# A selective scan's operands: the state as the inner partition index, and dt stored beside dt times x

## The chip, the cores and the metric

The kernel runs on one core of one Trainium2 chip. The metric is device time in microseconds (us) from one launch to its end; the median of the runs is given. Engine names are those of the profile: PE is the matrix engine (PEld its weight loads), DVE the vector engine, ACT the scalar engine, POOL the general-purpose engine, SP the engine whose queue issues nearly all DMAs here.

## The reference, cut to what matters

Two layers work on x of 4 batches by 48 x 48 tokens by 128 channels, all in float32. The first is a two-dimensional selective scan. After a group norm, an input projection to 256 channels, a 3 x 3 depthwise convolution and a SiLU, the tokens are scanned in K = 4 directions (rows, columns, and both backwards), with N = 16 states for each channel:

```python
x_dbl = jnp.einsum('bkdl,kcd->bkcl', xs, x_proj_w)
dts_r, Bs, Cs = (x_dbl[:, :, :R], x_dbl[:, :, R:R + N], x_dbl[:, :, R + N:])
dts = jnp.einsum('bkrl,kdr->bkdl', dts_r, dt_proj_w)
dt = jax.nn.softplus(dts + dt_proj_b[None, :, :, None])
A = -jnp.exp(A_logs).reshape(K, d, N)
...
def step(h, inp):
    dt_l, u_l, B_l, C_l = inp
    dA = jnp.exp(dt_l[..., None] * A)
    h = h * dA + (dt_l * u_l)[..., None] * B_l[:, :, None, :]
    y = jnp.einsum('bkdn,bkn->bkd', h, C_l)
    return (h, y)
```

The four directions' y are added, normed, gated and projected back to 128 channels. The second layer is an attention of the 2304 tokens with themselves, and then a mixture of four spectral convolutions over time (16 filters, the "STU").

## The kernel before, in words

**Tiling of the scan.** One batch is 4 directions x 6 chunks of CS = 384 tokens, 24 chunks (`Chunk`, L327). In a chunk, 256 channels x 16 states = 4096 scans are to be made. They are cut into 8 units (`Unit`, L437): h in 0..1 is the half of the channels, q in 0..3 a group of four states. A unit is a tile s of 128 partitions x 4 groups g x 384 tokens. Its 128 partitions are C4 = 4 states (c) times DL = 32 channels (j), and g runs over four sets of 32 channels. In the kernel before, partition p is c * 32 + j: the state is the outer index.

**Operands of a unit.** A channel's dt and dt * x are needed on four partitions, one for each state c; a state's B and C are needed on 32 partitions, one for each channel j. They are spread so:

- `prep` (L348) projects x to xd (dt's low-rank part, B, C), computes dt by a matmul and a softplus into re[:, h, 0] (L389, L397), multiplies by x into re[:, h, 1] (L414), and writes re out to a DRAM tile dtdud: `store(h)` (L401) issues four DMAs, one for each g, each of 32 partitions. dtdud is laid out as half, channel j, dt or dt * x, group g, token.
- `load(h)` (L405) reads dtdud back into the tile rep, with four DMAs, one for each state c, each writing 32 neighbouring partitions with all that a channel j has: 2 x 4 x 384 values, 12 KB in one run.
- `fetch` (L429) reads one row of xd, which was written to DRAM (xdd, L392), into 32 neighbouring partitions of a tile bc, four DMAs for a tile. C is always spread this way, and B for the units that POOL enters.
- For the other units PE spreads B: `spread` (L445) multiplies xd by a matrix of ones and zeros, made once at L119 to L125.

**A unit's work.** `enter` (L451) makes s = rep[:, 1] * B, on DVE for five of the eight units and on POOL for three. `scan` (L459) does, for each g, dA = exp(A * dt) on ACT (L464) and the scan on DVE (L467). `times_c` (L470) multiplies by C on POOL. `sum_c` (L478) sums the four states of each channel by a matmul with csum, a 128 x 32 matrix made at L128.

**What sets the order.** The kernel is issued in an order written out by hand. `scans` (L518) goes over the 192 units of a batch; unit by unit it enters the next units, gives 15 steps of `prep` for chunks up to three ahead, and lets other work run in between in proportion to its columns of matmul: for batch 0 the mixing of the filters' weights (`mixture`, L813), and for batches 1 to 3 the STU of the batch before (`stu`, L908). That work reads large tiles tt of filter values (L954) and G of weights (L965). Between two scan stages come the scan's epilogue, the attention, and the next batch's projection and convolution. After batch 3 its STU runs alone. `begin_scans` (L502) prepares a batch's first chunk ahead of its stage. Nearly all DMAs are issued by SP, in the order of the program. They use eight completion semaphores in turn, and a DMA waits until the earlier user of its semaphore has landed, so that at most eight are under way. The tile rep has three buffers, each bc tile one, tt four.

Of the kernel before, what the change touches and what calls it, by code (L numbers as in the profile page):

```python
# [8 lines left out]
F32 = mybir.dt.float32  # L9
AF = mybir.ActivationFunctionType  # L10
ALU = mybir.AluOpType
AX = mybir.AxisListType
# [3 lines left out]
P = 128  # L16
# [3 lines left out]
D, NS, R, K = 256, 16, 8, 4  # L20
NH = D // P
CS = 384
SUB = 384
NT = L // P
G4, DL, C4, Q4 = 4, 32, 4, 4
# [29 lines left out]
def hybrid_kernel(ctx: ExitStack, tc: tile.TileContext, a: dict, out: bass.AP):  # L55
# [3 lines left out]
    nc = tc.nc  # L59
    ctx.enter_context(tc.manual_schedule())  # L60
    wp = ctx.enter_context(tc.tile_pool(name="w", bufs=1, side="left"))
    keep = ctx.enter_context(tc.tile_pool(name="keep", bufs=1, side="left"))
    res = ctx.enter_context(tc.tile_pool(name="res", bufs=1, space=DRAM))
    dram = ctx.enter_context(tc.tile_pool(name="dram", bufs=3, space=DRAM))
    bank = {}

    ident = wp.tile([P, P], F32, name="ident")
# [48 lines left out]
    onerow = wp.tile([P, 1], F32, name="onerow")  # L116
    nc.vector.memset(onerow, 0.0)

    spread = wp.tile([P, 2, Q4, C4, DL], F32, name="spread")  # L119
    nc.vector.memset(spread, 0.0)  # L120
    for v in range(2):
        nc.gpsimd.affine_select(onerow, onerow, pattern=[[0, 1]], compare_op=ALU.not_equal, fill=1.0,
                                base=-R - 64 * v, channel_multiplier=1)
        nc.gpsimd.affine_select(spread[:, v], spread[:, v], pattern=[[-C4, Q4], [-1, C4], [0, DL]],
                                compare_op=ALU.not_equal, fill=1.0, base=-32 - 64 * v, channel_multiplier=1)  # L125

    csum = wp.tile([P, DL], F32, name="csum")
    nc.vector.tensor_reduce(csum, ident.rearrange("p (c j) -> p j c", j=DL), AX.X, ALU.add)  # L128
    shift = wp.tile([P, 1], F32, name="shift")
    nc.vector.memset(shift, -SHIFT)  # L130
    carry = wp.tile([P, NH, Q4, G4], F32, name="carry")
# [36 lines left out]
    def prologue(b, pool, mm_tile):  # L168
# [116 lines left out]
        for i in range(n):  # L285
            enter(i)
# [30 lines left out]
    def in_order(t, k, lo, n):  # L317

        if k % 2 == 0:
            return t[:, lo // W:(lo + n) // W, :]  # L320
        return t.rearrange("p h w -> p w h")[:, lo // H:(lo + n) // H, :]

    def mm_tile(name):
        pool, tag = bank["mm"]
        return pool.tile([P, 512], F32, tag=tag, name=name)

    class Chunk:  # L327
# [20 lines left out]
        def prep(self, pool):  # L348

            k, name, xc = self.k, self.name, xcs[self.b]
            xdd_ = xdd[k % 2][self.lo // CS]

            def rest(n=1):

                yield
                yield 0  # L360
                yield
                for i in range(3 * n - 3):
                    yield 0 if i % 3 == 1 else None

            if k >= 2:
                xd = self.xd = pool.xd.tile([P, CS], F32, tag="xd", name=f"xd{name}")
                nc.sync.dma_start(xd, xdd_)
            yield from rest(2)
            yield
            if k < 2:  # L370
                xd = self.xd = pool.xd.tile([P, CS], F32, tag="xd", name=f"xd{name}")
                ps = mm_tile(f"xp{name}")
                for h in range(NH):
                    nc.tensor.matmul(ps[:, :CS], xw[:, h, k, :], in_order(xc[h], k, self.lo, CS),
                                     start=(h == 0), stop=(h == NH - 1))
            yield 2 * CS if k < 2 else 0
            yield
            if k < 2:
                nc.scalar.activation(xd, ps[:, :CS], AF.Identity, bias=onerow)
            yield from rest()  # L380

            re = pool.one.tile([P, NH, 2, CS], F32, tag="re", name=f"re{name}")
            for h in range(NH):
                yield
                ps = mm_tile(f"dt{name}_{h}")
                nc.tensor.matmul(ps[:, :CS], dtw[:, k, h * P:(h + 1) * P], xd, start=True, stop=True)
                yield CS
                yield
                nc.scalar.copy(re[:, h, 0], ps[:, :CS])  # L389
                if h == 0:  # L390
                    if k < 2:
                        nc.sync.dma_start(xdd_, xd)  # L392
                    yield from rest()
            yield from rest()
            yield

            nc.scalar.activation(re[:, :, 0], re[:, :, 0], AF.Softplus)  # L397
            yield 0
            d = dram.tile([NH, DL, 2, G4, CS], F32, tag="dtdu", name=f"dtdud{name}")

            def store(h):  # L401
                for g in range(G4):
                    nc.sync.dma_start(d[h, :, :, g], re[g * DL:(g + 1) * DL, h])

            def load(h):  # L405
                rep = pool.rep.tile([P, 2, G4, CS], F32, tag="rep", name=f"rep{name}_{h}")
                for c in range(C4):
                    nc.sync.dma_start(rep[c * DL:(c + 1) * DL], d[h])
                self.rep.append(rep)

            for h in range(NH):
                x = in_order(xc[h], k, self.lo, CS)
                dt, dx = [re[:, h, i].rearrange("p (r w) -> p r w", w=x.shape[2]) for i in range(2)]
                nc.vector.tensor_tensor(dx, dt, x, ALU.mult)  # L414
            yield
            yield
            store(0)
            yield 0
            store(1)
            yield  # L420
            yield from rest(2)
            load(0)
            yield from rest(2)
            yield
            yield 0
            load(1)
            yield

        def fetch(self, i, pool):  # L429

            t = self.bc[i] = pool.one.tile([P, CS], F32, tag=f"bc{i}", name=f"bc{self.name}_{i}")
            src = xdd[self.k % 2][self.lo // CS]
            for c in range(C4):
                row = 64 * (self.k // 2) + 32 + 4 * i + c
                nc.sync.dma_start(t[c * DL:(c + 1) * DL], src[row].partition_broadcast(DL))

    class Unit:  # L437

# [6 lines left out]
        def spread(self, ps):  # L445

            self.bt = ps.tile([P, 512], F32, tag="B", name=f"B{self.name}")
            nc.tensor.matmul(self.bt[:, :CS], spread[:, self.ch.k // 2, self.q].rearrange("p c j -> p (c j)"),  # L448
                             self.ch.xd, start=True, stop=True)

        def enter(self, pool):  # L451

            full = self.full = pool.tile([P, G4, CS + 1], F32, tag="s", name=f"s{self.name}")
            s = self.s = full[:, :, self.ch.at]
            bt = self.ch.bc[self.q] if self.pool else self.bt[:, :CS]
            eng = nc.gpsimd if self.pool else nc.vector
            eng.tensor_tensor(s, self.ch.rep[self.h][:, 1], bt.unsqueeze(1).to_broadcast([P, G4, CS]), ALU.mult)  # L457

        def scan(self, g, dAs):  # L459
            ch = self.ch  # L460
            if g == 0:
                nc.scalar.copy(self.full[:, :, ch.slot], none if ch.first else carry[:, self.h, self.q])
            dA = dAs[g % 2]
            nc.scalar.activation(dA[:, 1:CS + 1], ch.rep[self.h][:, 0, g], AF.Exp,  # L464
                                 scale=A[:, ch.k, self.h * G4 + g, self.q:self.q + 1])
            s = self.full.rearrange("p g t -> p (g t)")[:, ch.scanned(g)]
            nc.vector.tensor_tensor_scan(s, dA[:, CS + 1:0:-1] if ch.rev else dA[:, :CS + 1], s, 0.0,  # L467
                                         ALU.mult, ALU.add)
# [49 lines left out]
    def scans(b, chunks, preps, front, sp, back, work, work_cols):  # L518
# [41 lines left out]
        for t in dAs:  # L560
            nc.vector.memset(t[:, 0:CS + 2:CS + 1], 0.0)
        spread(0)
        enter(-2)
        enter(-1)
        spread(1)
        for s in range(len(units) + 2):
            real = s < len(units)
# [340 lines left out]
    def stu(b, pool, ps):  # L908
# [162 lines left out]
        def ended(n, p, lo, hi):  # L1071
            t = now.pop(("T", n - KF + 1))[:hi - lo]
            nc.vector.tensor_tensor(t, t, p[:hi - lo], ALU.add)
            nc.sync.dma_start(out[b, 4 * lo:4 * hi].rearrange("(p j) c -> p j c", j=4), t)

        fetch(0, convs)
        for n, (_, k) in enumerate(items):
            if k == 0:
                begin(n)
            for i, (c, g) in enumerate(convs):  # L1080
                yield from conv(n, c, g)
                fetch(n, convs[i:])
                if i == 0:
                    fetch_G(n)
                elif i == 2 and n > 0:
                    yield from project(n - 1)
                elif i == 5 and k == 0:
                    if n > 0:
                        yield from end(n - 1)
                    yield from ar(n)  # L1090
# [157 lines left out]
```

## Time and profile before

| What | us |
|---|---|
| median of 3 runs | 6303.13 (6301.25 to 6308.65) |
| the profiled execution | 6311.58 |
| its span, first to last instruction | 6309.8 |
| PE busy | 5345.6 (85%) |
| DVE busy | 4482.0 (71%) |
| POOL busy | 3639.1 (58%) |
| ACT busy | 3039.2 (48%) |
| first scan stage, with the mixing of weights | about 140 to 1165 |
| scan stages mixed with the STU | about 1440 to 2540, 2840 to 3960, 4260 to 5370 |
| closing stage, STU alone | about 5660 to 6309 |

A busy time is the sum of an engine's instructions; it doesn't say which engine a stage waits for. The stages have different limits, so they are read one by one. In the whole program the DMA queue that SP feeds moved 1020.80 MB in 652032 packets, and the packets' time is 62.6% of 16 DMA engines over the span. In a line of waits, "A <- B: 30.4, 12, 5.2" says that A's engine sat idle until B for 30.4 us in all, 12 times, at the longest 5.2 us. The chain that ended last is followed back from the last instruction, each step to what released it.

### The profile page before, as it was taken

The numbers are of one execution on the slowest core, as the hardware profiler recorded it, in microseconds if no ns is written. First come the engines' busy times: TensorE is split into PE (matmuls) and PEld (weight loads), VectorE is DVE, ScalarE is ACT, GpSimd is POOL, SyncE is SP. The second block draws the span as 40 slices with busy tenths as digits, with TensorE's granted clock in tenths as the row PEclk, the third lists the DMA queues.
The fourth block names the chain that finished last, engine by engine and source line by source line (L and its number), as shares of the span: only waits on it lengthen the run. The fifth ranks groups of instructions, "written<-read, shape, count | busy, mean of one in ns | idle before, by whom it ended". The sixth has DMA issues, their size and how long they took to land.

```text
span 6309.8 us, 75729 instructions
## 1 busy us (share of the span) xinstructions
PE 5345.6 (85%) x24776; PEld 3339.5 (53%) x24776; DVE 4482.0 (71%) x5563; ACT 3039.2 (48%) x6429; POOL 3639.1 (58%) x1825
## 2 busy tenths in 40 slices
PE   3666666797999998888999998888999998889999
PEld 1222222444556666545555666545555666558889
DVE  6898989558889997458898997458889997311000
ACT  2665666245656654245555654245556654232111
POOL 1888888306788886206787886206788887200000
PEclk6877777799999999899999999899999999899999
DMA  4556555127888888128888888128888888026546
GB/s 100 133 142 148 143 141 143 41 57 179 204 208 222 222 223 236 48 64 192 196 216 209 222 225 230 45 64 194 194 216 214 221 227 236 30 65 159 159 140 215
DMA packets 658249, 1028.95 MB, mean 163 GB/s; under 512 B 93856, under 2 KB 515872, under 8 KB 633248
## 3 DMA queue, kind: packets, MB, share of 16 engines
q1 hardware_dynamic: 652032, 1020.80, 62.6%
q10 hardware_dynamic: 5824, 3.30, 0.2%
q8 instruction: 198, 3.24, 0.2%
q14 instruction: 195, 1.60, 0.1%
HBM read 905.79 MB, written 117.98 MB: 162 GB/s over the span
## 4 chain that ended last, share of the span: by engine, by line
PE 46%; DVE 20%; DMA 18%; ACT 5%; issue 4%; SPq 3%; POOL 3%; DVEq 0%; ACTq 0%; POOLq 0%
PE cv L984 21%; DVE s L467 8%; DMA tt<-fd 7%; PE pr L1050 5%; DVE s L457 4%; PE y L484 4%; PE s L726 3%; DMA rep<-dtdud 3%; DMA G<-gd 3%; PE o L719 3%; DMA bc<-xdd 3%; PE op L662 2%; PE B L448 2%; POOL s L476 2%; DVE xc L266 2%
## 5 line engine op out<-in xcount | busy, mean ns | idle before, releaser
L467 DVE TENSOR_TENSOR_SCAN s<-dA,s 128x385 f32<-128x385 f32 x3072 | 2761.5, 944 | 335.9 <-ACT dA L464 334.5
L476 POOL TENSOR_TENSOR s<-s,bc 128x1536 f32<-128x1536 f32 x768 | 2440.1, 3179 | 194.5 <-DVE s L467 107.6
L464 ACT ACTIVATE dA<-rep,A 128x384 f32<-128x384 f32 x3072 | 1780.1, 585 | 1289.3 <-DVE s L467 1256.2
L984 PE MATMUL cv<-tt,u 128*128 128x256 f32 (+3 forms) x7680 | 1656.8, 355 | 160.3 <-DMA tt<-fd 90.5
L984 PEld LDWEIGHTS cv<-tt,u 128*128 128x128 f32 x7680 | 1271.9, 193 | 662.1 <-issue 292.1
L457 POOL TENSOR_TENSOR s<-rep,bc 128x1536 f32<-128x1536 f32 x288 | 994.1, 3452 | 95.7 <-DMA bc<-xdd 95.7
L457 DVE TENSOR_TENSOR s<-rep,B 128x1536 f32<-128x1536 f32 x480 | 833.9, 1737 | 107.5 <-PE B L448 72.4
L984 PE MATMUL cv<-tt,us 128*128 128x256 f32 (+3 forms) x3840 | 862.5, 353 | 21.6 <-DMA tt<-fd 20.6
L484 PE MATMUL y<-s,csum 128*32 128x384 f32 x6144 | 722.0, 545 | 108.5 <-DVE ya L490 73.4
L984 PEld LDWEIGHTS cv<-tt,us 128*128 128x128 f32 x3840 | 646.9, 193 | 221.7 <-issue 82.9
L1013 DVE TENSOR_TENSOR U<-cv,Q 128x256 f32<-128x256 f32 (+1 forms) x640 | 245.5, 384 | 688.1 <-PE cv L984 678.5
L1050 PE MATMUL pr<-U,G 128*128 128x288 f32 (+7 forms) x2048 | 596.1, 422 | 11.0 <-DMA G<-gd 9.3
L448 PE MATMUL B<-xd,spread 128*128 128x384 f32 x960 | 443.7, 547 | 182.6 <-DVE s L457 170.6
L1010 ACT COPY U<-cv 128x256 f32<-128x256 f32 (+1 forms) x640 | 223.3, 349 | 643.6 <-PE cv L984 642.9
L475 POOL COPY carry<-s 128x4 f32<-128x4 f32 x640 | 121.4, 190 | 680.5 <-DVE s L467 652.2
L1050 PEld LDWEIGHTS pr<-U,G 128*128 128x128 f32 x2048 | 339.9, 192 | 158.6 <-issue 81.5
L998 ACT COPY Q<-cv 128x256 f32<-128x256 f32 (+3 forms) x640 | 223.4, 349 | 387.2 <-PE cv L984 384.8
L726 PE MATMUL s<-xnT 128*128 128x512 f32 (+1 forms) x720 | 357.8, 582 | 42.7 <-ACT xnT L688 23.4
L728 ACT ACTIVATE e<-s,shift 128x512 f32<-128x512 f32 (+1 forms) x360 | 231.2, 644 | 314.2 <-PE s L726 313.7
L160 POOL TENSOR_TENSOR ln_vu<-ln_vu,mhalf 128x4 f32<-128x4 f32 (+1 forms) x20 | 26.8, 1341 | 602.0 <-DVE ln_vu L159 602.0
L484 PEld LDWEIGHTS y<-s,csum 128*32 128x32 f32 x6144 | 127.3, 112 | 461.5 <-issue 333.4
L719 PE MATMUL o<-e,xn 128*128 128x512 f32 (+1 forms) x720 | 343.6, 560 | 4.5 <-ACT e L728 4.5
(161 smaller groups left out, 3722.7 us busy)
## 6 DMA issues: line engine op xcount, KB each, us to landing
rep<-dtdud SPq DMA_DIRECT2D x768, 384.0 KB, 7.6
tt<-fd SPq DMA_DIRECT2D x192, 577.0 KB, 5.2
bc<-xdd SPq DMA_DIRECT2D x2304, 48.0 KB, 3.4
tt<-fd SPq DMA_DIRECT2D x192, 513.0 KB, 4.8
tt<-fd SPq DMA_DIRECT2D x192, 385.0 KB, 4.5
dtdud<-re SPq DMA_DIRECT2D x768, 96.0 KB, 2.2
G<-gd SPq DMA_DIRECT2D x192, 256.0 KB, 5.6
tt<-fd SPq DMA_DIRECT2D x64, 514.0 KB, 5.9
```

Of the source, the lines that this page charges most:

```text
L448: nc.tensor.matmul(self.bt[:, :CS], spread[:, self.ch.k // 2, self.q].rearrange("p c j -> p (c j)"), self.ch.xd, start=True, stop=True)
L457: eng.tensor_tensor(s, self.ch.rep[self.h][:, 1], bt.unsqueeze(1).to_broadcast([P, G4, CS]), ALU.mult)
L464: nc.scalar.activation(dA[:, 1:CS + 1], ch.rep[self.h][:, 0, g], AF.Exp, scale=A[:, ch.k, self.h * G4 + g, self.q:self.q + 1])
L467: nc.vector.tensor_tensor_scan(s, dA[:, CS + 1:0:-1] if ch.rev else dA[:, :CS + 1], s, 0.0, ALU.mult, ALU.add)
L476: nc.gpsimd.tensor_tensor(self.s, self.s, ch.bc[Q4 + self.q].unsqueeze(1).to_broadcast([P, G4, CS]), ALU.mult)
L484: nc.tensor.matmul(ch.y[g * DL:(g + 1) * DL, :CS], csum, self.s[:, g], start=(self.q == 0), stop=(self.q == Q4 - 1))
L719: nc.tensor.matmul(po[J][:, :w], xn[:, i], e[:, :w], start=(i == 0), stop=(i == NT - 1))
L726: nc.tensor.matmul(p[:, :w], xnT[:, i * P:(i + 1) * P], xnT[:, 512 * J:512 * J + w], start=True, stop=True)
L728: nc.scalar.activation(e[:, :w], p[:, :w], AF.Exp, bias=shift)
L984: nc.tensor.matmul(p2[:, :, at - first:], x, t[:, :, hi - 1 - at + J * P:end if end >= 0 else None:-1], start=(c < 2 and J == 0), stop=(J ...
L1013: nc.vector.tensor_tensor(dst, src, q, ALU.add)
L1050: nc.tensor.matmul(p[:, :, v0:v1], Gs[n][:, q, x, :], U[n][:, 4 * q:4 * q + 4, v0:v1], start=False, stop=(k == KF - 1 and q == 1 and v1 == w))
```

## The change

Partition p of a unit becomes 4 * j + c: the state is the inner index. So a spreading load for the state c writes the partitions c, c + 4, ... c + 124 (rep and bc alike). In DRAM, dtdud is laid out as half, group g, channel j, then dt and dt * x side by side, so that a channel's two rows are one run of 3 KB. A store of one half becomes one DMA of 128 partitions, and a load reads four runs of 3 KB for each channel. The tile rep has the group ahead of the dt or dt * x index. The constants spread and csum and the host's layout of A_logs follow the new order of partitions.

```diff
-    spread = wp.tile([P, 2, Q4, C4, DL], F32, name="spread")
+    spread = wp.tile([P, 2, Q4, DL, C4], F32, name="spread")
...
-        nc.gpsimd.affine_select(spread[:, v], spread[:, v], pattern=[[-C4, Q4], [-1, C4], [0, DL]],
+        nc.gpsimd.affine_select(spread[:, v], spread[:, v], pattern=[[-C4, Q4], [0, DL], [-1, C4]],
...
-    nc.vector.tensor_reduce(csum, ident.rearrange("p (c j) -> p j c", j=DL), AX.X, ALU.add)
+    nc.vector.tensor_reduce(csum, ident.rearrange("p (j c) -> p j c", j=DL), AX.X, ALU.add)
...
-            d = dram.tile([NH, DL, 2, G4, CS], F32, tag="dtdu", name=f"dtdud{name}")
+            d = dram.tile([NH, G4, DL, 2, CS], F32, tag="dtdu", name=f"dtdud{name}")
 
             def store(h):
-                for g in range(G4):
-                    nc.sync.dma_start(d[h, :, :, g], re[g * DL:(g + 1) * DL, h])
+                nc.sync.dma_start(d[h].rearrange("g j i t -> (g j) i t"), re[:, h])
 
             def load(h):
-                rep = pool.rep.tile([P, 2, G4, CS], F32, tag="rep", name=f"rep{name}_{h}")
+                rep = pool.rep.tile([P, G4, 2, CS], F32, tag="rep", name=f"rep{name}_{h}")
                 for c in range(C4):
-                    nc.sync.dma_start(rep[c * DL:(c + 1) * DL], d[h])
+                    nc.sync.dma_start(rep[c::C4], d[h].rearrange("g j i t -> j g i t"))
                 self.rep.append(rep)
...
-                nc.sync.dma_start(t[c * DL:(c + 1) * DL], src[row].partition_broadcast(DL))
+                nc.sync.dma_start(t[c::C4], src[row].partition_broadcast(DL))
...
-            nc.tensor.matmul(self.bt[:, :CS], spread[:, self.ch.k // 2, self.q].rearrange("p c j -> p (c j)"),
+            nc.tensor.matmul(self.bt[:, :CS], spread[:, self.ch.k // 2, self.q].rearrange("p j c -> p (j c)"),
...
-            eng.tensor_tensor(s, self.ch.rep[self.h][:, 1], bt.unsqueeze(1).to_broadcast([P, G4, CS]), ALU.mult)
+            eng.tensor_tensor(s, self.ch.rep[self.h][:, :, 1], bt.unsqueeze(1).to_broadcast([P, G4, CS]), ALU.mult)
...
-            nc.scalar.activation(dA[:, 1:CS + 1], ch.rep[self.h][:, 0, g], AF.Exp,
+            nc.scalar.activation(dA[:, 1:CS + 1], ch.rep[self.h][:, g, 0], AF.Exp,
...
-        "A_logs": i[l0 + "A_logs"].reshape(K, NH * G4, DL, Q4, C4).transpose(4, 2, 0, 1, 3).reshape(P, K, NH * G4, Q4),
+        "A_logs": i[l0 + "A_logs"].reshape(K, NH * G4, DL, Q4, C4).transpose(2, 4, 0, 1, 3).reshape(P, K, NH * G4, Q4),
```

## The prediction, on record before the changed kernel was run

> **What bounds the kernel now.** I read the page first, for the chain that ended last and for the sizes of the transfers that the change touches.
>
> ```profile
> PE 46%; DVE 20%; DMA 18%; ACT 5%; issue 4%; SPq 3%; POOL 3%; DVEq 0%; ACTq 0%; POOLq 0%
> ...
> rep<-dtdud SPq DMA_DIRECT2D x768, 384.0 KB, 7.6
> ...
> bc<-xdd SPq DMA_DIRECT2D x2304, 48.0 KB, 3.4
> ...
> dtdud<-re SPq DMA_DIRECT2D x768, 96.0 KB, 2.2
> ```
>
> Transfers and the SP queue make 21% of the chain. The change touches three of them and, by the order of instructions in the two built programs, nothing else: PE, DVE, ACT and POOL run the same instructions in the same order. Next, busy time by stage: the first batch's scan stage, then the three in which scans run mixed with the spectral convolution of the batch before (from the second column: length, PE, PE weight load, DVE, ACT, POOL; at the end the clock, the DMA engines' share and GB/s).
>
> ```profile
> 140.00:1165.00 1025.00, 641.91 (x2461) 222.41 (x2462) 914.44 (x986) 607.33 (x1228) 873.16 (x425) 0.77 0.58 140
> ...
> 1440.00:2540.00 1100.00, 1015.93 (x5293) 664.63 (x5293) 968.07 (x1133) 635.41 (x1391) 867.99 (x420) 0.97 0.84 215
> ...
> 2840.00:3960.00 1120.00, 1019.91 (x5311) 665.10 (x5312) 973.72 (x1139) 638.17 (x1397) 871.54 (x422) 0.97 0.83 212
> ...
> 4260.00:5370.00 1110.00, 1019.82 (x5310) 665.25 (x5310) 973.58 (x1139) 638.53 (x1397) 871.29 (x422) 0.97 0.84 214
> ```
>
> The first stage is DVE's (914 of 1025), with 111 us idle. The mixed ones are PE's, which idles 84, 100 and 90 us: 274 in all is the most that faster transfers could give there. DMA is busy for 0.84 of them, so a load waits behind others. The waits of the first mixed stage (us in total, times, longest), PE and DVE first, then the SP queue's own:
>
> ```profile
> DVE s L467 <- ACT dA L464: 81.2, 96, 3.0
> ...
> PE cv L984 <- DMA tt<-fd: 30.4, 12, 5.2
> ...
> SPq L435 <- DMA rep<-dtdud: 81.5, 67, 2.9
> SPq L435 <- DMA tt<-fd: 38.1, 41, 2.3
> SPq L408 <- DMA tt<-fd: 35.8, 34, 3.0
> ```
>
> PE's largest single wait is for tt, which the change doesn't touch but which shares the 16 DMA engines and the SP queue with rep. The queue's waits for a DMA are the program's own: eight completion semaphores go round, so a DMA is issued only when the eighth before it has landed. They sum to 240 us of this stage. Its chain by line, with 27% of 1100 us in transfers:
>
> ```profile
> by line: PE cv L984 23.4%; DMA tt<-fd 12.7%; DVE s L467 6.6%; PE y L484 6.5%; PE pr L1050 6.3%; DMA G<-gd 6.1%; DVE s L457 4.9%; DMA bc<-xdd 4.3%; DMA rep<-dtdud 3.6%; PE B L448 3.4%; issue 2.9%; DVE re L414 2.2%; PE dt L386 1.8%; POOL s L4
> ```
>
> Last, windows in which one kind of transfer has the engines nearly to itself: rep at the start, tt in the closing stage (last columns: DMA share, GB/s).
>
> ```profile
> 114.00:116.00 2.00, 0.00 (x0) 0.00 (x0) 2.00 (x2) 0.00 (x0) 0.00 (x0) 0.50 1.02 215
> 116.00:118.00 2.00, 0.00 (x0) 0.00 (x0) 0.23 (x3) 0.00 (x0) 0.00 (x0) 0.50 1.05 227
> ...
> 6254.00:6255.00 1.00, 1.00 (x11) 1.00 (x10) 0.00 (x0) 0.27 (x1) 0.00 (x0) 1.00 1.03 373
> 6257.00:6258.00 1.00, 0.96 (x9) 0.77 (x7) 0.00 (x0) 0.15 (x2) 0.00 (x0) 1.00 0.95 365
> ```
>
> This is the heart of it: with all engines busy, rep moves 215 to 227 GB/s and tt 365 to 373. rep writes 32 neighbouring partitions in runs of 12 KB, tt all 128 in runs of about 2 KB. So long runs don't help, and something in where rep writes costs 40% of the rate.
>
> [...]
>
> **The change part by part.**
>
> 1. Spread loads of rep (768, 192 per batch). Runs go from 12 KB to 3 KB, partitions from 32 neighbours to every fourth. The new rate isn't in the trace: from 215 (no gain) to tt's 365. I take 330, a little under tt[...]. Per stage 192 x 393 KB = 75.5 MB: 351 us of all engines at 215, 229 at 330. That is 122 us, 0.11 of a 1100 us stage.
>
> 2. Fetches of bc (576 per batch, same size, same runs, every fourth partition). 28.3 MB, 132 us at 215, 86 at 330. The trace never shows them alone with full engines, so the gain lies between 0 and 46 us; I take 23, or 0.02. The share in a mixed stage falls from 0.84 to about 0.71.
>
> 3. Stores to dtdud: 192 per batch become 48 of 384 KB over 128 partitions. Each issue now takes 594 ns (median), 114 us of SP per batch; 48 of between 302 (the fastest rep issue) and 594 ns are 14 to 29, so about 90 us of SP go, and 144 turns of the eight semaphores. A rep issue is now 413 ns for a two-dimensional pattern; the three-dimensional one may cost what a store's did, 594, so 0 to 35 us come back per batch, and I take 17. SP is 70 us lighter per stage. It is in order, so tt and bc behind stores go out sooner.
>
> 4. What reads the tiles. dA's exp reads the same 384 contiguous values, the product at L457 four runs of 384 instead of one of 1536 at 1731 ns (480 on DVE, 834 us); B's operand there is broken into runs of 384 already. I take 0; 1% either way would be 8 us. csum, spread and A are set up once, at the same sizes: 0, and what hides them is the 95 us prologue.
>
> Now the path. In a mixed stage the chain holds transfers of 12.7% tt, 6.1% G, 4.3% bc and 3.6% rep: 140, 67, 47 and 40 us. tt lands in 5.7 us there and in 4.1 in the closing stage without scans (medians), G in 6.1 and 4.7; removing about a sixth of the traffic's engine time should close half of that, 14% and 11%: 20 and 7 us. rep lands in 7.6; its queued part shrinks with the rate, 28%: 11. bc 23%: 11. SP's share of the stores gives some 10. Sum 59 us. Next in line stands PE's own work with 84 us of slack, and DVE behind it with 132, so I let half through: 30 us per stage, 90 for three.
>
> The first scan stage: DMA is 0.58 busy there and DVE has the chain; rep 2.4%, the mixture's M 4.0%, SP at the stores 2.2% of 1025 us. 28% of 25, 20% of 41 and three quarters of 22 are 7 + 8 + 17 = 32; half, 16. Before its first scan everything waits in a line:
>
> ```profile
> 103.59 5.18 SPq L403 DMA_DIRECT2D dtdud<-re  x8
> 108.95 3.80 SPq L408 DMA_DIRECT2D rep<-dtdud  x8
> 113.77 20.56 SPq L435 DMA_DIRECT2D bc<-xdd  x24
> ```
>
> Two stores instead of eight save 4 us and the first rep group 2 to 3: 7 us. At the later stages the same load (13.6 us long) ends under attention's last matmuls, which hide it; without that cover it would be 6 us each. The closing stage and attention hold none of these transfers: 0.
>
> Sum: 90 + 16 + 7 = 113 us off the profiled execution's 6311.6 (span 6309.8): 6199. The median of the runs is 8.5 us lower than that execution: 6303 - 113 = 6190 us, -1.8%.
>
> **The rivals.** (A) The rate doesn't move[...]. Then only item 3 is left: 10 us per mixed stage, 8 in the first, 4 at the start: 42, so 6261. (B) DMA was the hidden bound of the mixed stages, and PE closes up: two thirds of 274 and 40 in the first, 223 us: 6080. For it: 27% of the chain; against it: PE's idle time is ended by DVE and ACT as well. (C) Slower: strided partitions or four times the packets make a rep load slower than now. A mixed stage spends 0.31 of its DMA time on rep at 215 GB/s and has 0.16 free; below 215 x 0.31/0.47 = 142 GB/s for rep DMA becomes the bound. At half of today's rate the share would be 1.15, each mixed stage 1270 us, and the kernel about 500 us slower, 6800. Against it: tt's shorter runs reach 365.
>
> **How the numbers follow.** Forecast (6130 to 6235): 0.62. A (6235 to 6300): 0.17. B (under 6130): 0.14. C: 0.07. A measurement of this kernel tells about 0.2% (13 us) from no change. A's upper end holds what is within that, 0.05; slower is C alone. The range from 6090 to 6290 leaves out C, B's far half and A's last part: 0.2.
>
> **What would show it.** rep alone at the start at over 300 GB/s with full engines says item 1 is right, 215 says A. The mixed stages' DMA share near 0.71, tt's landing under 5.3 us, SP's waits for DMAs well under 240 us per stage, PE's idle time down to about 60. It would be wrong if those waits shrink and the stages stay as long (DVE, ACT and PE hand each other the gap), or if rep's rate falls.

## The result, and the profile after

| | before | after |
|---|---|---|
| median | 6305.9 us | 6194.2 us |
| profiled execution | 6311.6 us | 6199.2 us |
| first scan stage, first to last scan | 1018 us | 1006 us |
| three mixed stages, likewise | 1105 + 1117 + 1107 = 3329 us | 1072 + 1080 + 1074 = 3226 us |
| first scan of all begins at | 124 us | 121 us |

The ratio is 0.9822 (95% interval 0.9805 to 0.9839); the median before is of four runs here, of three in the table ahead of the prediction. Of the 112 us between the two profiled executions, the mixed stages hold 103, the first scan stage 12 and the start 3; the rest (attention, closing stage) takes 6 back.

The page of the changed kernel, its chain and the three transfers (columns as before: count, KB each, median us to landing):

```profile
PE 53%; DVE 23%; ACT 8%; DMA 6%; issue 4%; POOL 3%; SPq 3%; DVEq 0%; ACTq 0%; POOLq 0%
...
rep<-dtdud SPq DMA_DIRECT2D x768, 384.0 KB, 5.3
...
bc<-xdd SPq DMA_DIRECT2D x2304, 48.0 KB, 2.9
...
dtdud<-re SPq DMA_DIRECT2D x192, 384.0 KB, 3.0
```

Transfers were 18% of the chain and are 6%, a share of the one chain that ended last and not time saved. The bytes are the same. Next the windows that answer to those of before: rep alone at the start, and the three mixed stages.

```profile
115.00:117.00 2.00, 0.00 (x0) 0.00 (x0) 0.74 (x1) 0.80 (x1) 0.00 (x0) 0.50 1.03 401
117.00:119.00 2.00, 0.93 (x2) 0.50 (x2) 1.01 (x1) 1.57 (x3) 0.00 (x0) 0.50 1.02 402
1432.00:2504.00 1072.00, 1007.31 (x5344) 662.40 (x5344) 971.41 (x1142) 641.05 (x1402) 872.96 (x422) 0.98 0.70 221
2806.00:3886.00 1080.00, 1012.72 (x5344) 664.91 (x5344) 971.26 (x1142) 640.86 (x1402) 872.37 (x422) 0.98 0.69 219
4189.00:5263.00 1074.00, 1010.93 (x5344) 663.12 (x5344) 971.40 (x1143) 641.18 (x1402) 873.13 (x422) 0.98 0.69 220
```

With all DMA engines busy rep now moves 401 GB/s, where it moved 215 to 227. The DMA engines' share of a mixed stage is 0.70, for the same bytes in less time. The waits of the first mixed stage, DVE and PE first, then SP's own:

```profile
DVE s L466 <- ACT dA L463: 74.1, 84, 3.0
...
PE cv L983 <- DMA tt<-fd: 7.5, 4, 2.6
...
SPq L953 <- PE cv L983: 263.3, 126, 6.3
...
SPq L434 <- DMA tt<-fd: 13.4, 20, 1.3
SPq L434 <- DMA rep<-dtdud: 9.4, 20, 0.7
```

PE's wait for tt has gone from 30 to 8 us, SP's waits for DMAs from 240 to 38 us in all. SP's longest wait is for PE to free a tt buffer, as it was before, but it has grown from 182 to 263 us: the loads of tt are issued as soon as there is room for them. In this stage tt lands in 4.7 us (5.6 before, medians), rep in 5.4 (7.6).

### The profile page after: what moved, and what is told of

Same layout as the page of the kernel before. It is cut to its first block, busy times and chain, and to the rows that moved or that the text cites. A ratio compares the mean times of both kernels' runs of the same rounds, so it can differ in the third digit from the quotient of the medians.

```text
span 6197.4 us, 74902 instructions
## 1 busy us (share of the span) xinstructions
PE 5306.5 (86%) x24776; PEld 3327.8 (54%) x24776; DVE 4476.8 (72%) x5563; ACT 3040.4 (49%) x6429; POOL 3638.0 (59%) x1825
## 4 chain that ended last, share of the span: by engine, by line
PE 53%; DVE 23%; ACT 8%; DMA 6%; issue 4%; POOL 3%; SPq 3%; DVEq 0%; ACTq 0%; POOLq 0%
PE cv L983 24%; DVE s L466 10%; PE pr L1049 6%; PE y L483 5%; DVE s L456 5%; PE s L725 4%; PE o L718 3%; ACT dA L463 2%; PE B L447 2%; PE op L661 2%; DVE xc L266 2%; DVE re L413 2%; POOL s L475 2%; DMA tt<-fd 2%; DMA rep<-dtdud 2%
## 5 line engine op out<-in xcount | busy, mean ns | idle before, releaser
L456 DVE TENSOR_TENSOR s<-rep,B 128x1536 f32<-128x1536 f32 x480 | 833.9, 1737 | 73.2 <-PE B L447 42.8
```

Of the source, the lines that this page charges most:

```text
L456: eng.tensor_tensor(s, self.ch.rep[self.h][:, :, 1], bt.unsqueeze(1).to_broadcast([P, G4, CS]), ALU.mult)
```

## The experiments

The theory: the DMA engine time that rep's loads no longer take is the gain, and it comes from the partitions that a load now writes, every fourth of the 128 instead of 32 neighbours. The rivals: the lighter store and the smaller number of DMAs; the avoiding of neighbours as such; bc. All ratios are to the kernel before, timed beside it. "Mixed" is the three mixed stages' length summed, 3329 us before and 3226 after. It is read from one profiled execution of each kernel: a second profile of the changed kernel has 3231, its first mixed stage 1084 us instead of 1072. So a few us of a sum, or ten of one stage, say nothing.

**The store and the layout alone.** The changed kernel's DRAM layout, with loads to neighbours as before (the constants go back with them; the lines are set against the changed kernel):

```diff
-                    nc.sync.dma_start(rep[c::C4], d[h].rearrange("g j i t -> j g i t"))
+                    nc.sync.dma_start(rep[c * DL:(c + 1) * DL], d[h].rearrange("g j i t -> j g i t"))
...
-                nc.sync.dma_start(t[c::C4], src[row].partition_broadcast(DL))
+                nc.sync.dma_start(t[c * DL:(c + 1) * DL], src[row].partition_broadcast(DL))
```

> The kernel before with dt and dt*x side by side, one store for each half and 3 KB runs, but the loads still write 32 neighbouring partitions. Theory (the gain is the rate at which rep and bc are written): rep stays near 215 GB/s, the DMA engines' share of a mixed stage stays above 0.80, SP's issue time falls by some 90 us per stage, and the time is 6255 to 6295. Rival (the gain comes from 576 fewer DMAs and a lighter SP queue): 6190 to 6225.

Measured: 6291.4 us, ratio 0.9958 (0.9943 to 0.9972). Rep alone at the start, then the first mixed stage, from its windows:

```profile
114.00:116.00 2.00, 0.00 (x0) 0.00 (x0) 0.00 (x0) 0.00 (x0) 0.00 (x0) 0.50 1.03 221
...
1436.00:2545.00 1109.00, 1024.38 (x5344) 668.46 (x5344) 972.53 (x1142) 641.18 (x1402) 873.54 (x422) 0.97 0.84 213
```

Rep keeps its old rate with runs of 3 KB, and the mixed stages keep nearly all of their length (3316 us). The first stage has 8 of its 12 us of gain (1010 us), and the first scan starts 3 us earlier, as after the change. So the part of the store and the layout is most of the first stage's gain and the start, and little of the mixed stages.

**The partitions alone.** The changed kernel with the old layout: four stores, runs of 12 KB (the tile rep and its readers follow).

```diff
-            d = dram.tile([NH, G4, DL, 2, CS], F32, tag="dtdu", name=f"dtdud{name}")
+            d = dram.tile([NH, DL, 2, G4, CS], F32, tag="dtdu", name=f"dtdud{name}")
...
-                nc.sync.dma_start(d[h].rearrange("g j i t -> (g j) i t"), re[:, h])
+                for g in range(G4):
+                    nc.sync.dma_start(d[h, :, :, g], re[g * DL:(g + 1) * DL, h])
...
-                    nc.sync.dma_start(rep[c::C4], d[h].rearrange("g j i t -> j g i t"))
+                    nc.sync.dma_start(rep[c::C4], d[h])
```

> The changed kernel with the old DRAM layout: four stores for each half, 12 KB runs, every fourth partition. Theory: rep reaches over 330 GB/s, the share of a mixed stage falls to about 0.70, and the time is 6195 to 6235, although SP issues 576 more DMAs. Rival (stores and SP): 6280 to 6320.

Measured: 6220.4 us, ratio 0.9847 (0.9832 to 0.9862).

```profile
118.00:120.00 2.00, 0.00 (x0) 0.00 (x0) 1.82 (x4) 1.68 (x2) 0.00 (x0) 0.50 1.00 424
1445.00:2524.00 1079.00, 1009.06 (x5344) 661.99 (x5344) 971.60 (x1142) 641.75 (x1402) 873.29 (x422) 0.98 0.72 219
```

The mirror image: the mixed stages have nearly all of their gain (3234 us), the first stage has none (1019). The two parts' ratios, 0.9958 and 0.9847, multiply to 0.981, which lies in the interval of the whole change. So they add, each in its own stages.

**Every second partition.** Is it enough that neighbours are avoided? Here partition 64 * (c // 2) + 2 * j + c % 2 holds state c and channel j; the constants follow. Of the two ranges expected, the first is for the case that avoiding neighbours isn't what counts.

```diff
-                    nc.sync.dma_start(rep[c::C4], d[h].rearrange("g j i t -> j g i t"))
+                    nc.sync.dma_start(rep[64 * (c // 2) + c % 2:64 * (c // 2) + 64:2], d[h].rearrange("g j i t -> j g i t"))
...
-                nc.sync.dma_start(t[c::C4], src[row].partition_broadcast(DL))
+                nc.sync.dma_start(t[64 * (c // 2) + c % 2:64 * (c // 2) + 64:2], src[row].partition_broadcast(DL))
```

> The changed kernel with partition 64*(c//2) + 2*j + c%2: a load writes every second partition of one half of the 128. [...]rep stays near 215 GB/s and the time is 6265 to 6330, a little worse than neighbours with the same stores since a strided issue takes longer on SP. If what counts is that neighbours are avoided, rep is above 330 GB/s and the time is 6190 to 6215.

Measured: 6300.5 us, ratio 0.9973 (0.9964 to 0.9982), mixed 3318 us. Rep at the start, two windows:

```profile
116.00:118.00 2.00, 0.00 (x0) 0.00 (x0) 0.00 (x0) 0.00 (x0) 0.00 (x0) 0.50 1.04 201
118.00:120.00 2.00, 0.00 (x0) 0.00 (x0) 0.30 (x1) 0.35 (x1) 0.00 (x0) 0.50 1.03 217
```

Strided, and no faster than neighbours: 201 to 217 GB/s, where neighbours had 215 to 227 in the kernel before and every fourth partition 401 to 424 (the change, and the partitions alone). So avoiding neighbours isn't what counts. What does isn't told apart: a load here also stays in one half of the 128 partitions, where the changed kernel's loads reach over both, and no run varies the step and the halves separately.

**The freed engine time filled again.** The changed kernel, with a transfer of 928 KB from SBUF to DRAM, which nobody reads, behind each group of rep loads:

```diff
                 self.rep.append(rep)
+                idle = dram.tile([P, IDLE], F32, tag="idle", name=f"idle{name}_{h}")
+                nc.sync.dma_start(idle, xc[h].rearrange("p h w -> p (h w)")[:, :IDLE])
```

> The changed kernel with one more transfer of 928 KB (128 partitions of xc written to DRAM, read by nobody) behind each group of four rep loads, 45.6 MB per batch, about what the faster rep and bc loads freed. SP issues only 192 DMAs more. Theory (DMA engine time is what was won): the share of a mixed stage is back above 0.80, tt lands in 5.3 us or more, and the time is 6250 to 6310. Rival (the gain is that rep and bc themselves land sooner): 6195 to 6225.

Measured: 6280.6 us, ratio 0.9949 (0.9930 to 0.9968).

```profile
1445.00:2538.00 1093.00, 1008.98 (x5344) 662.21 (x5344) 972.44 (x1142) 640.00 (x1402) 872.80 (x422) 0.98 0.80 256
...
PE cv L986 <- DMA tt<-fd: 27.3, 12, 5.4
```

With the share at 0.80 the mixed stages take 3295 us: 69 of the 103 us are gone again. tt lands in 5.5 us and PE waits 27 us for it, although rep (5.8 us) still lands far sooner than in the kernel before. So most of the gain isn't rep's own earlier arrival; it is what else the DMA engines and the queue can do. The waits of the first mixed stage before agree: only SP's queue waits for rep there, none of the computing engines. The added transfers also hold one of the eight semaphores each for 8.4 us (median; in the traces of before and after, no DMA of SP is issued until the eighth before it has landed), and SP's waits for DMAs are back at 127 us; how much of the 69 us is DMA engine time and how much is this window of eight, the run doesn't separate, so the theory's first half is shown for the two together.

**Rep and bc apart.** In one kernel bc alone goes back to neighbours, in the other rep alone. The constants stay, so what goes back meets the wrong states or channels: these two compute other values than the reference, and serve for the time alone.

```diff
-                nc.sync.dma_start(t[c::C4], src[row].partition_broadcast(DL))
+                nc.sync.dma_start(t[c * DL:(c + 1) * DL], src[row].partition_broadcast(DL))
```

```diff
-                    nc.sync.dma_start(rep[c::C4], d[h].rearrange("g j i t -> j g i t"))
+                    nc.sync.dma_start(rep[c * DL:(c + 1) * DL], d[h].rearrange("g j i t -> j g i t"))
```

> The changed kernel with bc still written to 32 neighbouring partitions, so that the rows of B and C that bc holds meet the wrong states; rep as in the change. Theory (item 2, bc's faster writing is worth 0 to 46 us of engine time per batch, and a fetch's issue is back from 587 to 419 ns): within 15 us of the changed kernel, 6180 to 6210. Rival (bc is a good part of the gain): 6215 to 6250.

Measured: 6192.0 us, ratio 0.9807 (0.9792 to 0.9821). The changed kernel wasn't timed beside it there, so next are both of them and the second kernel on one chip:

> The changed kernel once more, as the measure beside the two others on one chip: 0.981 to 0.984 of the kernel before.

> The changed kernel with bc written to 32 neighbouring partitions (the rows that bc holds meet the wrong states), timed beside the changed kernel. Theory: bc's faster writing and its slower issue cancel, so within 0.2% of the changed kernel. Rival: bc's writing is worth something by itself, over 0.2% slower.

> The changed kernel with rep written to 32 neighbouring partitions (the channels that rep holds meet the wrong states), bc as in the change. Theory (nearly all of the gain in the mixed stages is rep's): 6275 to 6320, a little slower than with both on neighbours, since bc's strided issue stays. Rival (bc's share is half): 6235 to 6260.

Measured on one chip: changed 0.9819 (0.9805 to 0.9832), bc on neighbours 0.9819 (0.9806 to 0.9832), rep on neighbours 0.9962 (0.9949 to 0.9974; 6289.1 us, mixed 3307). All that the partitions bring is rep's, as far as the intervals tell. bc's part is nil in the time: the DMA engines' share of the first mixed stage is 0.72 without it and 0.70 with it, but each of its issues takes longer on SP, as the next lines show for the kernel before and after (min, median and max ns of an issue in the first mixed stage):

```profile
L435 SPq DMA_DIRECT2D bc<-xdd x552: 302/419/2125, 1474.0 to 2524.5; - x184
```

```profile
L434 SPq DMA_DIRECT2D bc<-xdd x552: 447/588/2233, 1457.8 to 2479.0; - x184
```

**Fewer issues.** Since an SBUF tile's partitions now run through j and c in the order of a source [j, c, token], one DMA of 128 partitions can fetch a bc tile, its DRAM side repeating four rows 32 times:

```diff
-            for c in range(C4):
-                row = 64 * (self.k // 2) + 32 + 4 * i + c
-                nc.sync.dma_start(t[c::C4], src[row].partition_broadcast(DL))
+            row = src[64 * (self.k // 2) + 32 + 4 * i]
+            nc.sync.dma_start(t, bass.AP(row.tensor, row.offset, [[0, DL], [CS, C4], [1, CS]]))
```

> The changed kernel with each bc tile fetched by one DMA of 128 partitions instead of four strided ones: 1728 DMAs fewer in all, some 250 us of issue time less on SP per batch, the same bytes. Theory (engine time is what matters, SP has slack: it waits only 38 us for DMAs in a mixed stage): a small gain at the starts and in the first stage, 6165 to 6195. Rival (SP's issue is the bound by now): 6110 to 6160.

Measured: 6167.6 us, ratio 0.9769 (0.9753 to 0.9785).

```profile
1423.00:2487.00 1064.00, 1003.52 (x5344) 659.13 (x5344) 970.51 (x1142) 641.44 (x1402) 873.29 (x422) 0.99 0.69 222
```

It is about 0.5% better than the changed kernel by their ratios, and 0.4% better than the kernel with bc on neighbours, which was timed on the same chip. The first stage takes 998 us, the mixed ones 3202, and SP waits 7 us for DMAs in the first mixed stage. So SP's load counts a little: some 23 us in the mixed stages, for about 250 us of issue time less in each. The run also takes three of four turns of the eight semaphores from bc, and doesn't separate the two.

The same for rep, which then needs runs of 12 KB and four stores:

```diff
-                for c in range(C4):
-                    nc.sync.dma_start(rep[c::C4], d[h])
+                src = d[h]
+                nc.sync.dma_start(rep.rearrange("p g i t -> p (g i t)"),
+                                  bass.AP(src.tensor, src.offset, [[G4 * 2 * CS, DL], [0, C4], [1, G4 * 2 * CS]]))
```

> As e8, and each half of rep loaded by one DMA of 128 partitions with 12 KB runs (each read four times in a row from DRAM), with four stores of 3 KB runs. [...]Theory: rep at about the 400 GB/s seen after the change, DMA share as in e8, 6160 to 6195. Rival (SP): 6100 to 6150.

Measured: 6174.0 us, ratio 0.9776 (0.9761 to 0.9790), not told apart from the one before. So for rep the single DMA brings nothing that these runs can tell. Its 1536 KB land in 8.7 us (median, first mixed stage).

## Why the prediction was right, point by point

**Item 1, the rate of rep.** The reading that carried it was two windows with full DMA engines, 215 GB/s for one load and 365 for another; that writing every fourth partition would lift the rate was my estimate, which nothing in the profile before showed. 330 was too careful: 401. Landing fell from 7.6 to 5.4 us, 29%, where 28% was taken. Rival A, that the rate doesn't move, is refuted by it.

**Item 2, bc.** The DMA engines' share, 0.02, came out as taken. The term was still wrong: a cost was missing. An issue rose from 419 to 588 ns, 552 x 0.169 = 93 us of SP in a stage, and the time shows no gain.

**Item 3, the store.** Its own part held: 338 ns an issue (median), about 92 us of SP less per stage. The sum "SP is 70 us lighter" failed. Rep's issues went from 413 to 603 ns (+35 us), a little over the upper bound taken, and bc's +93 us had no place in it. The issue times of the three, count by median in the first mixed stage, were 231 + 76 + 107 = 414 us and are 325 + 111 + 15 = 451: SP got 37 us heavier. The reason I gave, a third dimension, was wrong too. The issues of rep with the store and layout alone, and with the partitions alone:

```profile
L407 SPq DMA_DIRECT2D rep<-dtdud x184: 302/423/2472, 1443.8 to 2487.4; - x184
...
L408 SPq DMA_DIRECT2D rep<-dtdud x184: 447/592/1622, 1455.5 to 2473.4; - x184
```

Three dimensions to neighbours take 423 ns, two dimensions with a step 592. So what goes with the longer issue is the step over partitions. That the stores would give 10 us per mixed stage and 42 in all also failed: alone, store and layout gave 13 us in the three mixed stages together and 25 in the whole (ratio 0.9958).

**Item 4, the readers of rep.** DVE's product is unchanged: 833.9 us in both pages.

**The path.** 30 us for a mixed stage were forecast, and 33, 37 and 33 came (21, 40 and 37 in the second profile of the changed kernel). The way there was partly luck. Transfers lost far more of the chain than I took (18% to 6% of the span; tt's landing 5.6 to 4.7 us, where 4.9 was taken), and of the store's 10 us a stage only 4 were there; that half would get through was a guess, and it covered both. My ceiling was also read wrongly: it was PE's idle time, but of the 103 us only some 72 are idle time. The rest is busy time. The first mixed stage before, in the same bounds as the lines after the change:

```profile
1445.00:2551.00 1106.00, 1021.09 (x5344) 668.34 (x5344) 973.77 (x1143) 640.47 (x1402) 874.45 (x422) 0.97 0.84 214
```

The same 5344 matmuls were busy for 1021 us and are for 1007, and the granted clock went with it. By the clock records of the two traces, PE ran at half its clock for 192 us of the three mixed stages before and runs so for 126 after. The matmul at L484 takes 847 ns in such stretches and 487 outside them (medians, before). If half of the stretches is counted as lost (an estimate from the clock records), 33 us of the difference are the clock's; PE's busy time of the three stages fell by 32, from 3063 to 3031 us. The two agree within 2 us. What brings the clock down no run isolates. In these two traces each half-clock stretch that begins inside a mixed stage, 40 before and 30 after, begins within 3 us of the end of a pause of PE of 0.9 us or more, where a moment taken at random does so in 19% of cases before and 15% after. Whether the shorter waits brought the clock's 33 us too isn't shown; the prediction has no term for them. Of its 30 us for a stage some 24 came as idle time; that the sum fits is in part this missing term. With the added traffic PE idles 84 us of the first mixed stage (85 before, 65 after), while its busy time, 1009 us, and its clock, 0.98, stay close to the changed kernel's.

**The first stage and the start.** 16 + 7 forecast, 12 + 3 measured. The start's line is shorter by 5 us from the product at L414 to the first scan, but the work before it ended 2 us later in this execution.

**Rivals B and C.** PE didn't close up: it still idles some 65 us in a mixed stage, and the chain is now PE's and DVE's, 76% of the span. The loads themselves were not slower: in the first mixed stage rep lands in 5.4 us (7.6 before, medians), bc in 3.3 (3.9), tt in 4.7 (5.6). What got slower, the issue, lies mostly in SP's slack: the issues that one DMA for each bc tile saves were worth about 0.5%.

## What to carry to other kernels

Compare transfers by their GB/s in windows where all DMA engines are busy. Here rep lagged there, 215 to 227 beside 365 to 373 for tt, with no other load landing in the window; so what held it back wasn't other traffic. It was the partitions it wrote (401 to 424 with every fourth), and the index order of a tile's partitions decided that. Then ask who is queued behind it: with the freed engine time filled again, 69 of the 103 us were gone, though rep still landed in 5.8 us instead of 7.6, so the gain came less from the faster load than from the other loads it stopped delaying. Compare PE's busy time only together with its clock (3063 us with 192 at half clock, 3031 with 126). An order that lets one DMA fill all 128 partitions saves issues too; for bc that was worth about 0.5% here, for rep nothing that could be told.

## What the runs showed of the hardware

- A DMA whose SBUF side steps over partitions took 166 to 179 ns longer to issue on SP (medians, first mixed stage): 419 to 588 ns for bc with step four, 585 with step two, at the same shape; 413 to 592 ns for rep at the same runs.
- 32 partitions with a step of four were written at up to 401 to 424 GB/s in windows of 2 us, more than the 365 to 384 of tt with 128 partitions and shorter runs in its best windows of 1 us. With a step of two inside one half it was 201 to 217, with neighbours 201 to 227.
- A DMA of 128 partitions that carries four times the bytes of a bc fetch took 553 ns to issue (median), less than one strided quarter of it (588).
- SP's DMAs, 5344 before and 4768 after, used eight completion semaphores. In both traces none was issued before the eighth ahead of it had landed, and at most eight were under way.
- PE's busy time for the same matmuls went with the granted clock: 3063 us in the three mixed stages with 192 us at half clock, 3031 with 126. Each of the 70 half-clock stretches that began there came with a pause of PE (0.9 to 5.2 us) that ended within 3 us of its begin.
